# Strassen's algorithm for the memory side of the gate in a gated cross-attention kernel on one Trainium2 core

## The chip, the core and the metric

The kernel runs on one of the eight cores of one Trainium2 chip. A core has five engines that run beside each other and meet only through semaphores: TensorE (PE: matrix products and transposes into PSUM; its weight loads are shown as PEld), VectorE (DVE), ScalarE (ACT), GpSimd (POOL) and SyncE (SP, which here only issues DMAs). Each engine works through its own instructions in order, and so does the DMA queue of each. The metric is the device time of one execution in microseconds (us).

## The reference

```python
# x: (8, 1024, 1024)   memory (ctx_1024): (8, 64, 512)
memory_proj = einsum('bme,de->bmd', memory, W_mem)              # called mp below
scores = einsum('bnd,bmd->bnm', x, memory_proj) / sqrt(1024)
attn = softmax(scores, axis=-1)
memory_context = einsum('bnm,bmd->bnd', attn, memory_proj)
gate_input = concatenate([x, memory_context], axis=-1)
gate = sigmoid(einsum('bnf,df->bnd', gate_input, W_gate) + b_gate)
fused = x + gate * memory_context
out = fused * rsqrt(mean(fused**2, axis=-1) + 1e-6) * norm_w
```

All is float32. The kernel splits W_gate into W1 (the columns that meet x) and W2 (those that meet memory_context). As memory_context is attn times mp, its part of the gate is attn times (mp @ W2.T), so the kernel computes mp @ W2.T + b_gate once for all 8 x 64 = 512 memory rows, and calls it mg.

## The kernel before

**Setup** (lines 116 to 452), once. Five matmuls of zeros occupy TensorE until the first data is there. SP issues the loads in this order: mem in two tiles of 256 rows (`memq`), the rest of W_mem (`wm`; its first chunk is issued by ACT), the eight row chunks of W2 (`w2`), the bias, and W1 in two halves (`w1_0`, `w1_1`). TensorE transposes the first `memq` tile into PSUM (`transpose_mem`, line 182), DVE and ACT copy it to `memT`, and TensorE forms the first half-width products with W_mem for four of the eight output chunks (`mem_product` with 256 columns); then the same for the second tile, then the rest of W_mem's product at 512 columns. The eight results `pm` fill the eight PSUM banks. DVE copies each to `mpT` (line 237): mp transposed, features on partitions, 512 memory rows in the free dimension.

mp goes out to DRAM twice, to be loaded again per batch: as rows (`mgd[0]`, by DVE block transposes into `mpq` and 16 DMAs, lines 240 to 254) and transposed (`mpd`, lines 255 and 256). Then TensorE computes mp @ W2.T as 2 column halves x 4 row tiles, each a sum over 8 chunks (`pg`, lines 429 to 434). DVE adds the bias to each tile, and SP stores it to `mgd[1]`. Beside these eight tiles, DVE also forms the sums of W1's blocks (`w1_tasks`) and the first block of rows of x, transposed (`first`); POOL does only the `inner_s` sums of the first product.

**W1's sums.** x @ W1.T is done by Strassen's algorithm (Winograd's form) on two levels. The outer level has the products 1 to 7, in the order 1, 6, 7, 5, 4, 2, 3 (`ORDER`, line 465). Their right operands are blocks 1, 7, 2, 3 of W1 and three outer sums, blocks 5, 6, 4 (`outer_sum`, 128x2048 elements each). Inside each block there is a second level, which needs four sums of 128x512 (`inner_sums`). In the kernel before, those of blocks 1, 7, 5, 6, 4 are made in the setup, and those of blocks 2 and 3 in slots 2 to 13 of the loop (line 501).

**Loop** (lines 747 to 750): 16 blocks of 512 rows of x, each 49 slots, and seven outer products of seven inner products each. An inner product is a slot: two matmuls of 128x256. The order of everything else is written out by hand: `at(slot, ...)` puts work in front of a slot's matmuls, and `mid((q, o), ...)` puts it behind a product's fifth inner product. Each outer product uses five PSUM banks, A to E, and F takes B's. DVE empties B, C and D into `u`, and at the end adds the inner results into `gate` (`fin`); POOL does the additions that need no PSUM (`pre`) and the left operands' sums (`inner_s`). The banks rotate from product to product:

```python
banks = [banks[i] for i in (2, 3, 0, 4, 1)]
```

so the next product's A is the old C, its B the old D, and its C the old A. In products 5, 4, 2 and 3 the attention's part of the gate is added in the same banks.

All instructions of an engine stay in the order in which the program issues them (`keep_in_program_order`). Tiles with the same tag share a buffer: the next user waits until the last reader is done.

Of the kernel before, what the change touches and what calls it, by code (L numbers as in the profile page):

```python
# [8 lines left out]
F32 = mybir.dt.float32  # L9
AF = mybir.ActivationFunctionType  # L10
ALU = mybir.AluOpType
# [4 lines left out]
P = 128  # L16
# [4 lines left out]
def tile_gated_cross_attention_rmsnorm(  # L21
# [7 lines left out]
    norm_w: bass.AP,  # L29
    out: bass.AP,  # L30
):

# [28 lines left out]
    nc = tc.nc  # L63
# [8 lines left out]
    H = 512  # L72
# [17 lines left out]
    def mm(o, lhsT, rhs, start, stop):  # L90
        pin(nc.tensor.matmul(o, lhsT, rhs, start=start, stop=stop, skip_group_check=True))  # L91

    def tt(eng, o, a, b, op):
        pin(eng.tensor_tensor(o, a, b, op))  # L94

    def load(o, i):
        pin(nc.sync.dma_start(o, i))

    def t4k(pool, shape, tag, name):
        return pool.tile(shape, F32, tag=tag, name=name)  # L100

    def rows_by_chunk(w, n):

        return w.rearrange("(p j) f -> p j f", j=n)

    def chunks(t, n):

        return t.rearrange("p s e -> p (s e)").rearrange("p (m j) -> p j m", j=n)
# [3 lines left out]
    def bank(n, shape, name):  # L112
        return ps.tile(shape, F32, tag=banks[n % 5], name=name)
# [20 lines left out]
    for k in range(KD):  # L134
        t = t4k(*((gpool, [P, D], "gate") if k < 7 else (apool, [P, D], "s4")), f"w2_{k}")
        load(t, w2r[:, k, :])
        w2.append(t)
    bias_sb = t4k(small, [P, D], "junk", "bias_sb")
    load(bias_sb, b_gate.partition_broadcast(P))

    w1 = [const.tile([P, 4, D], F32, name=f"w1_{h}") for h in range(2)]
    for h in range(2):
        load(w1[h], rows_by_chunk(w_gate_t[:D, :], KD)[:, 4 * h : 4 * h + 4, :])
    xq = {}

    def load_xq(q):
        b, n0 = q // QPB, (q % QPB) * QT
        xq[q] = t4k(xqpool, [P, 16, Q4], "xq", f"xq{q}")  # L150
        src = x[b, n0 : n0 + QT, :].rearrange("(s c) (i e) -> i c s e", c=32, i=4)
        for i in range(4):
            load(xq[q][32 * i : 32 * (i + 1), :, :], src[i])
# [3 lines left out]
        o: w1[h][:, :, c * H : (c + 1) * H]  # L157
        for o, h, c in ((1, 0, 0), (7, 0, 1), (2, 1, 0), (3, 1, 1))
    }
    for o in (5, 6, 4):  # L160
        outer_b[o] = const.tile([P, 4, H], F32, name=f"t{o}")
    inner_t = {o: const.tile([P, 3, 2, C], F32, name=f"it{o}") for o in range(1, 8)}

    def w_op(o, s):
        if s >= T4:
            return inner_t[o][:, s - T4, :, :]
        k, n = {R11: (0, 0), R21: (1, 0), R12: (0, 1), R22: (1, 1)}[s]
        return outer_b[o][:, 2 * k : 2 * k + 2, n * C : (n + 1) * C]

    nw_sb = const.tile([P, D], F32, name="nw_sb")  # L170

    ident = const.tile([P, P], F32, name="ident")
    make_identity(nc, ident)
# [3 lines left out]

    mpd = dram.tile([P, KD, BM], F32, name="mpd")
    mgd = dram.tile([2, BM, D], F32, name="mgd")
    memT = [t4k(apool, [P, 2, BM], f"a1{i + 1}", f"memT{i}") for i in range(2)]  # L180

    def transpose_mem(g):

# [11 lines left out]
            o = memT[k // 2][:, k % 2, cols]  # L195
            pin((nc.scalar.copy if k % 2 else nc.vector.tensor_copy)(o, pt[k][:, cols]))

    mpT = [
        t4k(rot, [P, 2, BM], tag, f"mpT_{tag}_{i}")
        for tag in ("l2", "u")  # L200
        for i in range(2)
    ]

    def mp_rows(j, q):
        return mpT[j // 2][:, j % 2, q * P : (q + 1) * P]


    mpq = [t4k(apool, [P, 4, Q4], f"a{i}{j}", f"mpq{i}{j}") for i in (1, 2) for j in (1, 2)]
    pt = [bank(4, [P, BM], "pt0")]
    pt += [ps_ctx.tile([P, BM], F32, tag="ctx", name=f"pt{k}") for k in (1, 2)]  # L210
    pt += [ps.tile([P, BM], F32, tag="sc", name="pt3")]
    pm = [bank(j, [P, BM], f"pm{j}") for j in range(4)]

    def mem_product(j, k, cols=slice(0, BM)):
        mm(
            pm[j][:, cols],
            chunks(wm[:, k : k + 1, :], KD)[:, j],
            memT[k // 2][:, k % 2, cols],
            k == 0 and cols.start == 0,
            k == KE - 1,  # L220
        )


    for g in range(2):
        transpose_mem(g)
        for j in range(KD // 2):
            mem_product(j, 0, slice(g * (BM // 2), (g + 1) * (BM // 2)))
    pm.append(bank(4, [P, BM], "pm4"))
    pm += [ps_ctx.tile([P, BM], F32, tag="ctx", name=f"pm{j}") for j in (5, 6)]
    pm += [ps.tile([P, BM], F32, tag="sc", name="pm7")]  # L230
    for j in range(KD // 2, KD):
        mem_product(j, 0)
    for k in range(1, KE):
        for j in range(KD):
            mem_product(j, k)
    for j in range(KD):
        pin(nc.vector.tensor_copy(mpT[j // 2][:, j % 2, :], pm[j]))
    load_xq(0)
    load(nw_sb, norm_w.partition_broadcast(P))
    for g in range(4):  # L240
        for j in range(0, KD, 2):
            pin(
                nc.vector.transpose(
                    chunks(mpq[g], KD)[:, j : j + 2],
                    mpT[j // 2][:, :, g * P : (g + 1) * P],
                )
            )
        for i in range(4):
            load(
                mgd[0, g * P : (g + 1) * P, i * Q4 : (i + 1) * Q4].rearrange(  # L250
                    "(s c) e -> c s e", c=32
                ),
                mpq[g][32 * i : 32 * (i + 1), :, :],
            )
    for j in range(0, KD, 2):
        load(mpd[:, j : j + 2, :], mpT[j // 2])


    def outer_sum(o, a, b):
        tt(nc.vector, outer_b[o], outer_b[a], outer_b[b], ALU.subtract)  # L260

    def inner_sums(o):
        for s, a, b in ((T1, R12, R11), (T2, R22, T1), (R12, R22, R12), (T4, R21, T2)):
            yield lambda s=s, a=a, b=b: tt(
                nc.vector, w_op(o, s), w_op(o, a), w_op(o, b), ALU.subtract
            )


    w1_tasks = [
        lambda: outer_sum(5, 7, 1),  # L270
        *inner_sums(1),
        lambda: outer_sum(6, 3, 5),
        lambda: outer_sum(7, 3, 7),
        *(f for o in (7, 5) for f in inner_sums(o)),
        lambda: outer_sum(4, 2, 6),
        *(f for o in (6, 4) for f in inner_sums(o)),
    ]
    w1_last = [f for o in (2, 3) for f in inner_sums(o)]


    A, S, L2, O = {}, {}, {}, {}
    sTs, attns, attnTs, scs, mps, mgs = {}, {}, {}, {}, {}, {}
    KH = KD // 2

    def where(q, t=0):
        return q // QPB, (q % QPB) * QT + t * P

    def transpose_x(q, t, half):

        key = q, t // 2, half  # L290
        if key not in A:
            A[key] = t4k(
                apool, [P, KH, 2 * P], f"a{t // 2 + 1}{half + 1}", f"a{t // 2 + 1}{half + 1}_{q}"
            )
        r = t % 2
        pin(
            nc.vector.transpose(  # L297
                A[key][:, :, r * P : (r + 1) * P],
                chunks(xq[q][:, 4 * t : 4 * t + 4, :], KD)[:, half * KH : (half + 1) * KH],
            )  # L300
        )

    def outer_s(q, n):
        a11, a12, a21, a22 = (A.get((q, r, h)) for r in range(2) for h in range(2))
        if n == 3:
            S[q, 3] = a21
            tt(nc.vector, a21, a11, a21, ALU.subtract)
            return
        s = S[q, n] = t4k(apool, [P, KH, 2 * P], f"s{n}", f"s{n}_{q}")
        if n == 1:  # L310
            tt(nc.vector, s, a21, a22, ALU.add)
        elif n == 2:
            tt(nc.vector, s, S[q, 1], a11, ALU.subtract)
        else:
            tt(nc.vector, s, a12, S[q, 2], ALU.subtract)
# [95 lines left out]
    def load_mp(b):  # L411
        mps[b] = t4k(small, [P, KD, M], "mpb", f"mpb{b}")
        load(mps[b], mpd[:, :, b * M : (b + 1) * M])

    def load_mg(b):
# [2 lines left out]
            load(mgs[b][g * M : (g + 1) * M, :], mgd[g, b * M : (b + 1) * M, :])  # L418


    first = [
        *(lambda t=t: transpose_x(0, t, 0) for t in (0, 1)),
        *(lambda t=t, h=h: transpose_x(0, t, h) for h in range(2) for t in (2, 3)),
        lambda: outer_s(0, 1),
        lambda: outer_s(0, 2),
        *(lambda t=t: transpose_x(0, t, 1) for t in (0, 1)),
    ]
    done, n = 0, 0
    for h in range(2):
        cols = slice(h * H, (h + 1) * H)  # L430
        for q in range(NPAIR):
            pg = bank(n, [P, H], f"pg2_{h}_{q}")
            for k in range(KD):
                mm(pg, mp_rows(k, q), w2[k][:, cols], k == 0, k == KD - 1)
            stage = t4k(small, [P, H], ("mg", "attnT", "mpb")[n % 3], f"g2_{h}_{q}")
            tt(nc.vector, stage, pg, bias_sb[:, cols], ALU.add)
            load(mgd[1, q * P : (q + 1) * P, cols], stage)
            if n < 5:
                while done < len(w1_tasks) * (n + 1) // 5:
                    w1_tasks[done]()  # L440
                    done += 1
            if n == 4:
                for f in first[:2]:
                    f()
                for part in range(2):
                    inner_s(0, 1, part)
            elif n == 5:
                for f in first[2:]:
                    f()
            n += 1  # L450
    load_mp(0)
    load_mg(0)


# [43 lines left out]
            at(t0 + 10, load_mp, (q + 1) // QPB)  # L498
            at(t0 + 49, load_mg, (q + 1) // QPB)

    for i, fn in enumerate(w1_last):
        at((2, 3, 4, 5, 10, 11, 12, 13)[i], fn)
    slot = 0

    def step():
# [274 lines left out]
```

## Time and profile before

Three runs: 989.25, 989.34 and 990.49 us, median 989.34. The profiled execution took 990.88 us; its span, from the first instruction to the last, is 989.1 us, and the granted TensorE clock 0.995 of full.

| stretch of the span, us | what TensorE does | DVE busy | POOL busy |
|---|---|---|---|
| 0 to 6.67 | zeros, and waits for mem | little | little |
| 6.67 to 12.3 | mem's transposes, first half-width products | 1.7 us | none |
| 12.3 to 38.4 | W_mem's product | idle 19.9 us before the first copy | none |
| 38.4 to 93.4 | mp @ W2.T | 4 to 5 of each 5 us from 35 to 65, then 3.2 to 5 up to 90 | from 88.5 only |
| 93.4 to the end | the loop, 16 x 56 us | 2.4 to 5 of each 5 us | 2.1 to 5 of each 5 us from 100 on |

The page gives the busy time of each engine and the chain of work that ended last: from the last instruction back to whatever released it. A line such as `38.58 54.93 PE pg L91 x128` reads: from 38.58 us on, for 54.93 us, 128 records of TensorE writing tile `pg`, recorded at line 91 (all matmuls go through one helper). A matmul on FP32 operands shows as two records. `[0.84 <-DMA memq<-in_mem]` at a line's end means that the engine had been idle for 0.84 us, and that this load ended the wait.

### The profile page before, as it was taken

To read this page: it belongs to the slowest core of one execution; us is meant where nothing else is said; L and a number is where in the kernel's file an instruction comes from. 1 tells how busy PE (TensorE), PEld (TensorE's weight loads), DVE (VectorE), ACT (ScalarE), POOL (GpSimd) and SP (SyncE) were. 2 spreads that over 40 slices of the span, in tenths; PEclk is the share of its full clock that TensorE was granted. 3 is DMA by queue.
4 is the path that set the end of the run, shared out by engine and by line. 5 is a ranking of instruction groups with operands and counts; after the bars stand their busy time and mean duration, and the time that the engine had idled before them with its cause. 6 is when DMAs were issued, how large, how long until landed. Compare 5 with 4: busy or idle time off the path is not lost.

```text
span 989.1 us, 14267 instructions
## 1 busy us (share of the span) xinstructions
PE 974.1 (98%) x4962; PEld 775.8 (78%) x4962; DVE 810.3 (82%) x1491; ACT 321.7 (33%) x592; POOL 688.1 (70%) x851
## 2 busy tenths in 40 slices
PE   9999999999999999999999999999999999999994
PEld 7545788888888888888887888888887888888873
DVE  0677787979798897979798897979797988979787
ACT  1000115233333415142342424152333334151434
POOL 0002777878787787878787887878787887868772
PEclk9999999999999999999999999999999999999998
DMA  9772537191926556281927465381918364472612
GB/s 367 200 239 71 90 58 167 54 202 64 168 80 130 125 119 148 71 188 61 182 85 130 115 127 131 85 192 48 197 65 154 103 137 109 102 176 66 169 65 85
DMA packets 69160, 126.76 MB, mean 128 GB/s; under 512 B 12384, under 2 KB 47200, under 8 KB 68704
## 3 DMA queue, kind: packets, MB, share of 16 engines
q1 hardware_dynamic: 60304, 93.86, 35.0%
q0 software_dynamic: 8640, 31.46, 17.3%
q8 instruction: 39, 0.64, 0.3%
q10 hardware_dynamic: 144, 0.52, 0.2%
q14 instruction: 33, 0.27, 0.1%
HBM read 85.98 MB, written 39.85 MB: 127 GB/s over the span
## 4 chain that ended last, share of the span: by engine, by line
PE 96%; DVE 2%; DMA 1%; issue 0%; ACT 0%; POOL 0%; DVEq 0%; ACTq 0%
PE kA L91 19%; PE pc L91 12%; PE kE L91 11%; PE kF L91 10%; PE kD L91 10%; PE kC L91 10%; PE kB L91 10%; PE psT L91 6%; PE pg L91 6%; PE pm L91 3%; DVE gate L94 1%; DMA memq<-in_mem 1%; DVE gate L594 0%; PE pa L391 0%; PE sc L365 0%
## 5 line engine op out<-in xcount | busy, mean ns | idle before, releaser
L94 POOL TENSOR_TENSOR gate<-gate,u 128x256 f32<-128x256 f32 x336 | 270.5, 835 | 123.3 <-DVE u L94 123.3
L94 POOL TENSOR_TENSOR l<-a 128x256 f32<-128x256 f32 x128 | 128.5, 1004 | 151.5 <-PE pg L91 87.1
L516 ACT ACTIVATE gate<-gate 128x512 f32<-128x512 f32 x128 | 79.2, 631 | 399.8 <-DVE gate L94 399.8
L297 DVE STREAM_TRANSPOSE a<-xq 128x512 f32<-128x512 f32 x128 | 138.0, 1100 | 0.0
L91 PE MATMUL pc<-mg,attnT 64*128 64x256 f32 x512 | 127.4, 389 | 0.0
L545 DVE SCALAR_TENSOR_TENSOR gate<-gate,ss,nw_sb 128x512 f32<-128x512 f32 x120 | 126.1, 1061 | 1.1
L91 PE MATMUL kB<-it,l 128*128 128x256 f32 x448 | 115.0, 379 | 0.0
L91 PE MATMUL kD<-it,l 128*128 128x256 f32 x448 | 115.0, 379 | 0.0
L91 PEld LDWEIGHTS pc<-mg,attnT 64*128 64x128 f32 x512 | 90.6, 186 | 29.7 <-issue 21.2
L91 PE MATMUL kA<-w,a 128*128 128x256 f32 x384 | 98.7, 379 | 0.4 <-ACT u L660 0.4
L91 PEld LDWEIGHTS kB<-it,l 128*128 128x128 f32 x448 | 85.1, 190 | 11.6
L91 PEld LDWEIGHTS kD<-it,l 128*128 128x128 f32 x448 | 85.1, 190 | 11.6
L94 DVE TENSOR_TENSOR gate<-gate,pc 128x512 f32<-128x512 f32 x128 | 87.3, 682 | 5.9 <-ACT gate L516 5.9
L660 ACT COPY u<-kA 128x256 f32<-128x256 f32 x112 | 40.6, 363 | 142.2 <-PE kA L91 140.0
L91 PEld LDWEIGHTS kA<-w,a 128*128 128x128 f32 x384 | 71.6, 190 | 10.2 <-ACT u L660 0.8
L94 POOL TENSOR_TENSOR l<-s 128x256 f32<-128x256 f32 x96 | 75.5, 786 | 1.6 <-PE kF L91 1.5
L94 DVE TENSOR_TENSOR u<-u,kB 128x256 f32<-128x256 f32 x112 | 45.6, 408 | 30.1 <-PE kB L91 26.0
L91 PE MATMUL kE<-it,a 128*128 128x256 f32 x256 | 69.0, 392 | 0.0
L91 PE MATMUL kA<-t,s 128*128 128x256 f32 x256 | 67.4, 386 | 0.0
L91 PE MATMUL kC<-w,l 128*128 128x256 f32 x256 | 65.7, 379 | 0.0
L91 PE MATMUL kF<-w,l 128*128 128x256 f32 x256 | 65.7, 379 | 0.0
L530 ACT ACTIVATE junk<-gate 128x1024 f32<-128x1024 f32 x60 | 63.6, 1060 | 1.6 <-DMA gate<-in_x 0.6
(107 smaller groups left out, 1959.5 us busy)
## 6 DMA issues: line engine op xcount, KB each, us to landing
xq<-in_x SPq DMA_DIRECT2D x64, 512.0 KB, 9.7
gate<-in_x POOLq DMA_DIRECT2D x60, 512.0 KB, 8.9
out<-gate SPq DMA_DIRECT2D x60, 512.0 KB, 2.6
w<-in_w_gate_t SPq DMA_DIRECT2D x8, 512.0 KB, 11.3
w<-in_w_gate_t SPq DMA_DIRECT2D x2, 2048.0 KB, 16.2
mg<-mgd SPq DMA_DIRECT2D x16, 256.0 KB, 4.1
mgd<-mpq SPq DMA_DIRECT2D x16, 128.0 KB, 2.7
mgd<-g SPq DMA_DIRECT2D x8, 256.0 KB, 2.2
```

What stands on the lines that cost most here:

```text
L91: pin(nc.tensor.matmul(o, lhsT, rhs, start=start, stop=stop, skip_group_check=True))
L94: pin(eng.tensor_tensor(o, a, b, op))
L297: nc.vector.transpose(A[key][:, :, r * P : (r + 1) * P], chunks(xq[q][:, 4 * t : 4 * t + 4, :], KD)[:, half * KH : (half + 1) * KH],)
L516: pin(nc.scalar.activation(g, g, AF.Sigmoid))
L530: nc.scalar.activation(junk, O[q, t], AF.Square, accum_out=ss[:, t % 2 : t % 2 + 1])
L545: nc.vector.scalar_tensor_tensor(g[:, cols], g[:, cols], rstd[:, t % 2 : t % 2 + 1], nw_sb[:, cols], ALU.mult, ALU.mult,)
L660: pin(nc.scalar.copy(p1, kb["A"]))
```

## The change

It does five things.

1. `mem` is wholly transposed before W_mem's product starts; that product then runs at 512 columns throughout. `memT` moves to other buffers.
2. `pm` is copied in two halves of 256 rows, one by DVE, one by ACT, into four tiles `mpT[r][h]` (row half r, feature half h: m11, m12, m21, m22).
3. mp @ W2.T is done by one step of Strassen's algorithm: seven products of 256x512 by 512x512, in the order 1, 6, 5, 2, 7, 4, 3. Each has two row tiles of four matmuls. W2's sums are t1, t2, then b12 and b21 in place; mp's are s1, s2, s3, and s2 once more. The results are combined in c11, c12, c21 and c22 on DVE. The bias is added once to c11, c12 and c21 (c22 takes it from c12) by POOL.
4. POOL also takes b12's sums, s3, the second s2, and the inner sums of W1's blocks 7 and 6. Those of blocks 5 and 4 move into the loop with those of 2 and 3: 16 sums in slots 3 to 23.
5. The loads of the bias and of norm_w are issued behind W1. The rows of mp are stored (`store_mp`) between the products, and `load_mp(0)` in their middle.

```diff
-    for g in range(2):
-        transpose_mem(g)
-        for j in range(KD // 2):
-            mem_product(j, 0, slice(g * (BM // 2), (g + 1) * (BM // 2)))
...
+    for g in range(2):
+        transpose_mem(g)
+    pm = [bank(j, [P, BM], f"pm{j}") for j in range(5)]
...
+    for k in range(KE):
+        for j in range(KD):
+            mm(
+                pm[j],
+                chunks(wm[:, k : k + 1, :], KD)[:, j],
+                memT[k // 2][:, k % 2, :],
...
-    for j in range(KD):
-        pin(nc.vector.tensor_copy(mpT[j // 2][:, j % 2, :], pm[j]))
...
-    for h in range(2):
-        cols = slice(h * H, (h + 1) * H)
-        for q in range(NPAIR):
-            pg = bank(n, [P, H], f"pg2_{h}_{q}")
-            for k in range(KD):
-                mm(pg, mp_rows(k, q), w2[k][:, cols], k == 0, k == KD - 1)
-            stage = t4k(small, [P, H], ("mg", "attnT", "mpb")[n % 3], f"g2_{h}_{q}")
-            tt(nc.vector, stage, pg, bias_sb[:, cols], ALU.add)
-            load(mgd[1, q * P : (q + 1) * P, cols], stage)
...
+    w2_sum(nc.vector, t1, b12, b11)
+    w2_sum(nc.vector, t2, b22, t1)
+    w2_sum(nc.gpsimd, b12, b22, b12)
+    w1_place(5)
+    outer_sum(5, 7, 1)
+    inner_sums(nc.vector, 1)
...
+    mpT = [[t4k(apool, [P, KH, HM], f"a{r + 1}{h + 1}", f"mpT{r}{h}") for h in range(2)] for r in range(2)]
+    for j in range(KD):
+        for r, copy in ((0, nc.vector.tensor_copy), (1, nc.scalar.copy)):
+            pin(copy(mpT[r][j // KH][:, j % KH, :], pm[j][:, r * HM : (r + 1) * HM]))
+    (m11, m12), (m21, m22) = mpT
...
+    def mg_product(n, l, r):
+        nonlocal mg_next
+        pgs = []
+        for t in range(2):
+            tag = mg_banks[mg_next % 8]
+            mg_next += 1
+            pg = (ps_ctx if tag == "ctx" else ps).tile([P, H], F32, tag=tag, name=f"pg{n}_{t}")
+            for k in range(KH):
+                mm(pg, l[:, k, t * P : (t + 1) * P], r[k], k == 0, k == KH - 1)
+            pgs.append(pg)
+        return pgs
...
+    def mg_sum(o, a, pgs):
+        for t in range(2):
+            tt(nc.vector, o[:, t, :], a[:, t, :], pgs[t], ALU.add)
...
+    s1 = mp_step(nc.vector, "s1", apool, m21, m22, ALU.add)
+    s2 = mp_step(nc.vector, "s2", apool, s1, m11, ALU.subtract)
+    outer_sum(7, 3, 7)
+    w1_place(7)
+    s3 = mp_step(nc.gpsimd, "l2", rot, m11, m21, ALU.subtract)
+    for n in range(4):
+        inner_sum(nc.gpsimd, 7, n)
...
+    pgs = mg_product(1, m11, b11)
+    for t in range(2):
+        pin(nc.scalar.copy(c11[:, t, :], pgs[t]))
+    store_mp(2)
+    store_mp(3)
+    pgs = mg_product(6, s2, t2)
+    mg_sum(c21, c11, pgs)
+    store_mp(0)
+    tt(nc.gpsimd, s2, m12, s2, ALU.subtract)
+    pgs = mg_product(5, s1, t1)
+    mg_sum(c12, c21, pgs)
+    mg_bias(nc.gpsimd, c12, 1)
+    store_mp(1)
+    w1_place(6)
+    outer_sum(6, 3, 5)
     load_mp(0)
+    pgs = mg_product(2, m12, b21)
+    mg_sum(c11, c11, pgs)
+    mg_bias(nc.gpsimd, c11, 0)
+    store_mg(c11, 0, 0)
+    w2_sum(nc.vector, b21, b21, t2)
+    w1_place(4)
+    outer_sum(4, 2, 6)
+    for n in range(4):
+        inner_sum(nc.gpsimd, 6, n)
+    pgs = mg_product(7, s3, b12)
+    mg_sum(c22, c12, pgs)
+    mg_sum(c21, c21, pgs)
+    store_mg(c22, 1, 1)
+    for t in range(2):
+        transpose_x(0, t, 0)
+    for part in range(2):
+        inner_s(0, 1, part)
+    for t in (2, 3):
+        transpose_x(0, t, 0)
+    pgs = mg_product(4, m22, b21)
+    mg_sum(c21, c21, pgs)
+    mg_bias(nc.gpsimd, c21, 0)
+    store_mg(c21, 1, 0)
+    for t in (2, 3):
+        transpose_x(0, t, 1)
+    outer_s(0, 1)
+    for t in range(2):
+        transpose_x(0, t, 1)
+    pgs = mg_product(3, s2, b22)
+    mg_sum(c12, c12, pgs)
+    store_mg(c12, 0, 1)
+    outer_s(0, 2)
     load_mg(0)
...
-    for i, fn in enumerate(w1_last):
-        at((2, 3, 4, 5, 10, 11, 12, 13)[i], fn)
+    for o in (2, 3):
+        w1_place(o)
+    for i, (o, n) in enumerate((o, n) for o in (5, 4, 2, 3) for n in range(4)):
+        at(
+            (3, 4, 5, 6, 10, 11, 12, 13, 14, 15, 17, 18, 19, 20, 22, 23)[i],
+            inner_sum,
+            nc.vector,
+            o,
+            n,
+        )
```

`w2_sum` is four subtractions of 128x512, one for each chunk; `mp_step` is one of 128x1024; `mg_bias` is two additions of 128x512; `store_mp(g)` is two DVE block transposes of 128x512 and four DMAs; `store_mg` is one DMA of 512 KB.

## The prediction

> **What bounds the kernel now.** I read the busy times first, then the chain that ended last, then that chain in order of time.
>
> ```profile
> span 989.1 us, 14267 instructions
> PE 974.1 (98%) x4962; PEld 775.8 (78%) x4962; DVE 810.3 (82%) x1491; ACT 321.7 (33%) x592; POOL 688.1 (70%) x851
> PE 96%; DVE 2%; DMA 1%; issue 0%; ACT 0%; POOL 0%; DVEq 0%; ACTq 0%
> ...
> 8.62 2.88 PE pm L91 x8
> 11.50 0.96 PE pt L189 x8
> 12.46 26.11 PE pm L91 x64
> 38.58 54.93 PE pg L91 x128
> 93.51 0.86 PE kA L91 x4
> ```
>
> The chain is TensorE for 96%; its own waits add up to 3.6 us in the whole run. So time goes only if TensorE loses work, and comes only if TensorE is made to wait. The change rewrites the stretch from 8.6 to 93.4 us. In it `pg` is a block without a gap: 54.93/128 = 0.429 us for each pass of 512 columns. An FP32 matmul is two records here, so one matmul costs 0.858 us.
>
> **Part 1: seven products for eight.** Before: 8 tiles x 8 matmuls = 64. After: 7 products x 2 row tiles x 4 = 56 of the same shape (128x128 against 512). 8 x 0.858 = **6.87 us** go, if the products follow each other. With T for the end of `pm`, product n starts at T + 6.87(n-1), and the loop at T + 48.1. Their inputs, laid out on DVE and POOL by rows of the trace (DVE sums 0.61 us apart for 128x512, about 1.15 for 1024 and 2.2 for 2048; stream transposes 1.02; sums with a PSUM input 0.61 to 0.68):
>
> - The W2 loads are ahead of W1 and bias in the queue and land by about 22 us (the last is issued near 11.7 and takes 10.2), so `t1` and `t2` (8 x 0.61) end near 23. `w1_0` is issued 1.2 us earlier (the bias load was in front) and lands near 26.8, not 28; then `outer_sum(5)` and the four sums of block 1 take 2.2 + 2.4, to 31.5. The first `pm` is ready to copy near 32, and DVE idled until 32.6 before: free. At 3 us later the `m11` copies would still be in time.
> - The eight copies (DVE 0.42, ACT 0.37, beside each other) keep up with one `pm` per 0.86 us. s1 and s2 are ready at T + 3; product 6 needs them at T + 6.9.
> - POOL has no 128x512 row; two 128x256 passes at their 0.69 spacing give 1.38, 1024 elements 2.76. s3 ends near T + 0.5 (needed T + 27.5), b12 before 30 us, the second s2 near T + 16.5 (needed T + 41.2).
> - The b21 sums on DVE start when product 2 ends (T + 27.5) and its sums are done, about T + 28.2, and end at T + 31 to 33; product 4 needs them at T + 34.4. This is the tightest on DVE.
> - Handover: `outer_sum(4)` ends near T + 33.5 to 35.5; POOL then has the four sums of block 6 (5.5), four sums of `inner_s(0,1)` (2.8), needed near T + 49, and done at T + 44. Queued behind them are c21's bias (2.8), its store (2.2 to landing for a smaller one; I take 2.5), and the `inner_s(0,6)` sums, which reuse c21's buffer: T + 50.4, needed T + 58.6.
> - DVE's `mg_sum(c12)`, `outer_s(0,2)` end near T + 51; the first DVE add of the loop could start at T + 49.8. The four slots until product F reads that bank again cover the 1.3 us, and DVE idled 1.47 us at the score product.
>
> DMA: SP waits in order for c11's bias, c22, c21, c12 and c12's landing before `load_mg(0)`, so the load of the next x goes out some 6 us into the loop, not 3.3. It takes about 10 us, and is used 26 us in. `load_mp` is past by T + 25. Nothing waits.
>
> **Part 2: mem transposed first.** Here the order of records matters.
>
> ```profile
> 6.67 1.95 PE L189 MATMUL pt<-ident,memq 128*128 128x128 f32 x8 [0.84 <-DMA memq<-in_mem]
> 8.42 3.08 PE L91 MATMUL pm<-memT,wm 128*128 128x256 f32 x8
> 11.34 1.13 PE L189 MATMUL pt<-ident,memq 128*128 128x128 f32 x8
> 12.30 26.28 PE L91 MATMUL pm<-memT,wm 128*128 128x256 f32 x64
> ```
>
> In windows of a tenth of a microsecond, transposes start 0.214 us apart up to 8.2, the half-width passes 0.43 apart up to 10.55 and 0.24 or less after that; the second transposes are 0.12 apart. The array runs at half pace until about 10.6, although the granted-clock row reads 1.0. After: the second memory tile landed at 1.2 + 6.6 = 7.8, so its eight transposes run from 8.4 at 0.214, to 10.1. Then 64 full passes, 64 x 0.429 = 27.5; half a microsecond at half pace costs 0.25. T = 10.1 + 27.5 + 0.25 = 37.8, against 38.42: **0.6 us** gained. The Trainium skill, "TensorE: Matmul & The Clock Gate", Part 1, says that the full clock comes after a busy window of 3.4 us that runs free of the kernel. By that, 10.6 can move by a window from run to run; by the row it stays. I keep the row, and 0 to 1.0 as ends.
>
> **Part 3: eight sums moved into the loop.** Blocks 5 and 4, eight sums of 128x512, leave the setup's DVE work; with blocks 2 and 3 there are 16 in slots 3 to 23, where 8 were in slots 2 to 13. The eight new ones are in slots 14 to 23, on a full DVE:
>
> ```profile
> 109.64 1.23 DVE L94 TENSOR_TENSOR w<-w 128x512 f32<-128x512 f32 x1
> 110.80 0.41 DVE L94 TENSOR_TENSOR gate<-gate,kE 128x256 f32<-128x256 f32 x1
> 111.13 0.88 DVE L94 TENSOR_TENSOR it<-w,it 128x512 f32<-128x512 f32 x1
> ...
> 112.93 0.41 DVE L94 TENSOR_TENSOR gate<-gate,kF 128x256 f32<-128x256 f32 x1
> 113.26 0.41 DVE L94 TENSOR_TENSOR u<-u,kB 128x256 f32<-128x256 f32 x1
> ```
>
> kF of product 6 ended about 109.5 and is evacuated at 112.93: DVE is some 3 us behind before anything is added. The four sums of slots 10 to 13 took 0.68, 0.79, 1.23 and 0.88, against 0.69 alone: mean 0.90, about 0.81 apart. Bank D of one outer product becomes bank B of the next. From 113.26 there are five adds at 0.34 to D's last, so 114.96, plus four new sums ahead of it. At 0.81 that is 118.2, and kB of product 5 wants the bank at 116.86: **1.3 us** of stall. From there to the same point of product 5 there are four more sums (3.2), five adds (1.7), the attention difference (0.4), two transposes (2.04) and four adds (1.3): 126.9. kB of product 4 wants it at 125.03 + 1.3 = 126.3: **0.6** more. After that DVE idles about 3 us between 128 and 133 and catches up. Together 1.9.
>
> A rule speaks against this part and against POOL's new share. "SBUF — State Buffer", Who interferes with whom: a DVE instruction with two SBUF inputs contends with a GpSimd one that reads SBUF, and whichever issues second is fully blocked. POOL is busy 4.24 and 4.92 us of 5 in 110:115 and 115:120. By the rule each new sum waits for half a POOL sum, 0.61 + 0.37 = 0.98, and the same count gives 2.0 + 1.3 = 3.3. At the uncontended 0.61 it gives 0.5. Part of the blocking is in this row, which comes from this very loop, so I take the row's 1.9 and keep 0 to 3.3. In the setup the rule bites little: `mg_sum` has a PSUM input and transposes have one input, so only c12's and c11's biases and c21's meet DVE sums, some 2 us later in all, inside the slacks above.
>
> **The sum.** 6.87 + 0.6 - 1.9 = 5.6 us less. The profiled execution took 990.88, span 989.1 and 1.8 around it: a span near 983.5. On the median of the runs, 989.34 - 5.6 = **983.7 us**.
>
> **Rivals.**
>
> A, likeliest, 0.60: as summed, 982.3 to 985.3.
>
> B, 0.17: the loop's added sums are hidden, because POOL and DVE interleave better than in slots 10 to 13; 989.34 - 7.5 = 981.9. For it: later blocks of rows run with extra norm instructions on DVE and TensorE hardly waits. Against: only about three of those fall in slots 0 to 24, and eight are added here.
>
> C, 0.13: the handover costs 2 us too, for instance b21 or c21's bias late, beside the dear end of Part 3: 989.34 - 7.5 + 5.3 = 987.1, spread from 985.3 to 989. For it: the tight b21 slack. Against: 4 to 8 us of slack elsewhere.
>
> D, 0.08, slower: POOL's chain at the handover. From T + 35.5 it does 12.4 us of sums at a stretch factor f and a store of 2.5 until `inner_s(0,6)`, so TensorE waits 12.4f - 20.6. This begins at f = 1.66; 7.5 us are eaten, the loop's loss aside, at f = 2.27, a 128x512 POOL sum of 3.1 us. At f = 2.5 it waits 10.4: 989.34 - 7.5 + 10.4 + 1.9 = 994.1. For it: single POOL sums of 1.64 beside a DVE sum, 2.4 times 0.69. Against: the worst group of POOL sums has a mean of 1004 ns, f = 1.45, and most DVE work at that place is transposes.
>
> E, 0.02: the products go no faster, because the passes lengthen with the new operands: 989. Against: the same shapes, and a weight load (0.19 us) under the 0.43 of a pass.
>
> **Numbers.** What a measurement here can tell from no change is about 0.2%, 2.0 us: under 987.4 is faster, over 991.3 slower. Faster: A, B and 0.09 of C = 0.86. Same: 0.04 of C and E = 0.06. Slower: D, 0.08. The range joins the ends, best start with nothing lost in the loop, 989.34 - 6.87 - 1.0 = 981.5, to C's middle, 987.1; a little wider, 981.2 to 987.3.
>
> **What would show it.** `pg` with 112 records at 0.429, without a gap; the loop's first kA near 85.9, not 93.35. `pm` starting near 10.1 as one run of 64 passes. TensorE waits of 0.5 to 3.3 us in outer products 5 and 4 of the first block of rows, with DVE adds as releasers, and none later. I am wrong if a product waits for POOL or for b21, if the first kB waits for `inner_s`, or if kB of product 5 finds its bank free.

## The result, and the profile after

The changed kernel takes **985.07 us** (median of 6 runs, 984.92 to 986.23) against 989.32 (6 runs beside it, 989.25 to 990.80): 4.25 us less, a ratio of 0.9956 with a 95% interval of 0.9943 to 0.9969. The profiled execution took 986.23 us, its span is 984.4, 4.7 less than before.

The page's first lines and its chain by engine, after:

```profile
span 984.4 us, 14254 instructions
PE 968.4 (98%) x4938; PEld 771.3 (78%) x4938; DVE 823.4 (84%) x1495; ACT 324.9 (33%) x602; POOL 722.2 (73%) x871
PE 95%; DVE 2%; POOL 1%; DMA 1%; issue 0%; ACT 0%; DVEq 0%; ACTq 0%
```

TensorE has 24 records less: 16 for the eight matmuls that went, 8 because mem's half-width products are whole. POOL is in the chain now with 1%, where it was at 0%. The chain in order of time shows where (start, length, what):

```profile
6.66 3.66 PE pt L196 x16
10.32 27.76 PE pm L92 x64
38.08 48.07 PE pg L92 x112
86.15 0.86 PE kA L92 x4
...
107.95 0.43 DVE u L95
108.37 0.07 issue
108.44 2.93 POOL gate L95 x3
111.37 1.14 POOL l L95
112.51 0.04 issue
112.55 1.13 PE kC L92 x4
...
116.60 4.17 POOL gate L95 x6
120.77 0.70 POOL l L95
121.51 1.13 PE kC L92 x4
```

`pg` is 48.07 us without a gap, where it was 54.93. At 86 us the changed kernel is 7.4 us ahead. Then the chain leaves TensorE twice in the first block of rows, for DVE and POOL, in products 7 to 4 of the loop. What TensorE itself waited for, in the whole run (total, times, longest):

```profile
PE kA L92 <- ACT u L740: 1.7, 3, 1.1
PE pz L92 <- DVE zeros L118: 1.2, 1, 1.2
PE kB L92 <- DVE gate L95: 0.9, 1, 0.9
PE pt L196 <- DMA memq<-in_mem: 0.8, 1, 0.8
PE kC L92 <- POOL l L95: 0.8, 2, 0.6
```

The third and fifth line are new. The table sets the same records of both profiles side by side (starts, us; the lead is the difference).

| record | before | after | lead |
|---|---|---|---|
| first `pg` | 38.42 | 37.92 | 0.50 |
| loop's first kA | 93.35 | 85.99 | 7.36 |
| product 7, kF | 115.14 | 107.98 | 7.16 |
| product 5, kB | 116.86 | 110.82 | 6.04 |
| product 5, kC | 117.72 | 112.55 | 5.17 |
| product 4, kB | 125.03 | 120.23 | 4.80 |
| product 4, kC | 125.89 | 121.51 | 4.38 |
| product 2, first kA | 132.34 | 128.06 | 4.28 |
| next block's scores | 154.81 | 150.53 | 4.28 |
| last block's scores | 925.46 | 921.18 | 4.28 |

So the setup gained 7.36 us, and 3.08 of them were lost again within 42 us of the loop, nothing after that until the last block. In that block 0.33 more went, and the time from the last DVE instruction's end to the end of the span is 0.7 shorter.

### The profile page after: what moved, and what is told of

Its sections match the earlier page's. It is cut to its first block, busy times and chain, and to the rows that moved or that the text cites. A ratio compares the mean times of both kernels' runs of the same rounds, so it can differ in the third digit from the quotient of the medians.

```text
span 984.4 us, 14254 instructions
## 1 busy us (share of the span) xinstructions
PE 968.4 (98%) x4938; PEld 771.3 (78%) x4938; DVE 823.4 (84%) x1495; ACT 324.9 (33%) x602; POOL 722.2 (73%) x871
## 4 chain that ended last, share of the span: by engine, by line
PE 95%; DVE 2%; POOL 1%; DMA 1%; issue 0%; ACT 0%; DVEq 0%; ACTq 0%
PE kA L92 19%; PE pc L92 11%; PE kE L92 11%; PE kD L92 10%; PE kC L92 10%; PE kF L92 10%; PE kB L92 9%; PE psT L92 6%; PE pg L92 5%; PE pm L92 3%; DVE gate L95 1%; POOL gate L95 1%; DMA memq<-in_mem 1%; DVE gate L674 0%; DVE u L95 0%
## 5 line engine op out<-in xcount | busy, mean ns | idle before, releaser
L92 PEld LDWEIGHTS kA<-w,a 128*128 128x128 f32 x384 | 71.6, 190 | 10.2 <-ACT u L740 0.8
## 6 DMA issues: line engine op xcount, KB each, us to landing
mpd<-mpT SPq DMA_DIRECT2D x4, 512.0 KB, 11.7
```

## The experiments

Each was run beside the kernel before, on one of two chips; that took 989.31 us in the median on the first and 989.20 on the second. The changed kernel was not run again there, so the differences from its 985.07 us are across chips. They are between medians unless a profile is named. The experiments ask three things: whether the added sums alone cost the 3 us, which of them and through which engine, and what the other parts were worth.

**The sums alone, in the kernel before.** The inner sums of blocks 5 and 4 leave the setup for the loop; nothing else is changed.

```diff
-        *(f for o in (7, 5) for f in inner_sums(o)),
+        *inner_sums(7),
         lambda: outer_sum(4, 2, 6),
-        *(f for o in (6, 4) for f in inner_sums(o)),
+        *inner_sums(6),
-    w1_last = [f for o in (2, 3) for f in inner_sums(o)]
+    w1_last = [f for o in (5, 4, 2, 3) for f in inner_sums(o)]
-        at((2, 3, 4, 5, 10, 11, 12, 13)[i], fn)
+        at((3, 4, 5, 6, 10, 11, 12, 13, 14, 15, 17, 18, 19, 20, 22, 23)[i], fn)
```

> The kernel before, with Part 3 alone: the inner sums of W1's blocks 5 and 4 leave the setup and go into slots 3 to 23 of the loop, as in the changed kernel. Theory (the eight added DVE sums alone cause the loop's loss): 989.3 + 3.1 = 992.4 us, with waits of TensorE at kB and kC of product 5 and at kC of product 4 in the first block of rows. Rival (the loss comes from how the new setup hands over to the loop: DVE late, POOL late, loads late): 989.3, no waits there.

Measured: 994.12 us median, 992.46 to 994.29; 1.0038 (1.0026 to 1.0051). Its runs fall in two groups, 992.5 to 992.7 and 994.1 to 994.3, and so do those of the kernel before, 989.2 to 989.3 and 990.5 to 990.8 (of which more below). Group against group the sums cost 3.3 to 3.5. The lower group lies where the theory put the time (992.4); the median is in the upper one because three of the five runs are. Its profile has the same waits as the changed kernel's:

```profile
PE kB L91 <- DVE gate L94: 0.9, 1, 0.9
PE pt L189 <- DMA memq<-in_mem: 0.8, 1, 0.8
PE kC L91 <- POOL l L94: 0.8, 2, 0.6
```

No part of the new setup is there, and the loss is. The handover is out as its cause.

**The sums of blocks 2 and 3 later**, in the changed kernel:

```diff
-            (3, 4, 5, 6, 10, 11, 12, 13, 14, 15, 17, 18, 19, 20, 22, 23)[i],
+            (3, 4, 5, 6, 10, 11, 12, 13, 22, 23, 29, 30, 31, 32, 33, 34)[i],
```

> The changed kernel, with the sums of blocks 2 and 3 in slots 22, 23 and 29 to 34, where DVE idled about 3 us before, and not in 14 to 23. Theory (the crowding in slots 14 to 23): the 3.1 us of waits in products 7, 5 and 4 go, 985.1 - 2.5 to 3.1 = 982.0 to 982.6; a new lag in product 2 could give a part back. Rival (handover): 985.1.

Measured: 982.34 us (982.11 to 982.50); 0.9925 (0.9912 to 0.9937). That is 2.7 us below the changed kernel: the same sums, placed where DVE had idle time, are all but free. From the loop's first kA to the first kA of product 2 its profile takes 39.11 us; the kernel before takes 38.99 there and the changed kernel 42.07. TensorE's waits on DVE and POOL in the loop are gone from its profile. It beats both kernels.

**POOL's order.** In the first block of rows, the second half of `inner_s` for products 5 and 4 is put ahead of the additions that wait for DVE:

```diff
-            for part, t in ((0, 1), (1, 5)):
+            for part, t in ((0, 1), (1, 2 if q == 0 and i in (2, 3) else 5)):
```

> The changed kernel, with one edit in POOL's queue: in the first block of rows, the second half of inner_s for products 5 and 4 stands ahead of the pre additions (slots 16 and 23, not 19 and 26). Theory (part of the loss is POOL's order: those sums stand behind additions that wait for a late DVE): the waits of kC in products 5 and 4, 0.6 + 0.2 us in the records and about 1.3 to 1.7 in lost time, go, and the wait of kB (0.9) stays: about 983.6. Rival (only DVE's lag counts, POOL's order just shows it): 985.1, the time lost at kC comes back at another bank.

Measured: 984.89 us (984.83 to 985.00); 0.9951 (0.9937 to 0.9965): against 985.07, no change that can be told. TensorE's waits in it:

```profile
PE kB L92 <- DVE gate L95: 0.9, 1, 0.9
PE kF L92 <- DVE u L95: 0.5, 1, 0.5
PE kD L92 <- DVE u L95: 0.3, 1, 0.3
```

The wait for POOL is gone, and two waits for DVE stand in its place. From the loop's first kA to the first kA of product 2 it takes 126.70 - 84.63 = 42.07 us, and the changed kernel 128.06 - 85.99 = 42.07 as well. So the rival has the time right: the loss comes back at other banks. But the edit did not leave DVE alone. The second of the added sums took 1.10 us here, beside POOL's moved ones, and 0.69 in the changed kernel, and bank D of product 7 was empty 25.2 us into the loop, not 24.8. What POOL's order would be worth with DVE undisturbed is therefore open.

**Which four sums.** Two complements: block 2's sums late and block 3's left in place, and the other way round.

```diff
-            (3, 4, 5, 6, 10, 11, 12, 13, 14, 15, 17, 18, 19, 20, 22, 23)[i],
+            (3, 4, 5, 6, 10, 11, 12, 13, 29, 30, 31, 32, 19, 20, 22, 23)[i],
```

> The changed kernel, with block 2's four sums alone moved from slots 14, 15, 17, 18 to 29 to 32; block 3's stay in 19, 20, 22, 23. By the prediction's count (the four sums ahead of bank D's last add in product 7 are the costly ones): bank D is free at 114.96 on the old scale, before kB of product 5 asks for it at 116.86, D of product 5 at 123.7, before 125.03: no wait of TensorE in products 5 and 4, 982.3 us. Rival (any eight sums before slot 24 cost the same): half of the 2.7 us that late sums gave back, 983.7.

Measured: 982.22 us (982.11 to 983.15); 0.9930 (0.9917 to 0.9942). Banks D are free in time, as expected, but "no wait" is not quite so: kC of product 5 starts 1.16 us behind kB in its profile, and not 0.86, as its left operand comes late from POOL. The other:

```diff
-            (3, 4, 5, 6, 10, 11, 12, 13, 14, 15, 17, 18, 19, 20, 22, 23)[i],
+            (3, 4, 5, 6, 10, 11, 12, 13, 14, 15, 17, 18, 29, 30, 31, 32)[i],
```

> The complement: block 3's four sums moved from slots 19, 20, 22, 23 to 29 to 32; block 2's stay in 14 to 18. By the count: kB of product 5 still waits (1.3 us), kC of product 5 with it (about 0.9 more), product 4 no longer: 982.3 + 1.3 to 2.2 = 983.6 to 984.5. Rival (any eight sums cost the same): 983.7, as in the other one; then the two do not differ.

Measured: 983.76 us (983.71 to 984.73); 0.9946 (0.9934 to 0.9958). Its waits on the loop's banks:

```profile
PE kB L92 <- DVE gate L95: 0.9, 1, 0.9
PE kC L92 <- POOL l L95: 0.2, 1, 0.2
```

This time is that of the theory and of the rival alike; only the pair tells them apart. The two differ by 1.5 us, so the number of sums before slot 24 is not what counts. With four sums in slots 19 to 23 alone, the stretch from the loop's first kA to product 2 takes 39.38 us, 0.4 more than in the kernel before, and the time is that of the run with all eight late. Four in slots 14 to 18 cost 1.5 more, and those in 19 to 23 another 1.3 (985.07 - 983.76) once the first four have made DVE late.

**mem's transposes.** The old order is put back in the changed kernel:

```diff
     for g in range(2):
         transpose_mem(g)
+        for j in range(KD // 2):
+            mem_product(j, 0, slice(g * (BM // 2), (g + 1) * (BM // 2)))
...
+    for j in range(KD // 2, KD):
+        mem_product(j, 0)
+    for k in range(1, KE):
+        for j in range(KD):
+            mem_product(j, k)
```

> The changed kernel, with Part 2 undone: mem is transposed in two parts with half-width products of W_mem between them. Theory: pm ends at 38.4, not 37.9, and the time is 0.5 us longer, 985.6. Rival (the start's half-pace phase hides it): 985.1, no change.

Measured: 985.19 us (985.07 to 986.47); 0.9956 (0.9943 to 0.9968). Against 985.07 that is 0.1 us, within what the runs scatter. Neither expectation is excluded by its interval alone. The next part tells why the profile promised more.

**Full pace from the start.** The profiles taken in this case show two kinds of start. The chain's start in the changed kernel, and in the one with all eight sums late (start, length):

```profile
2.63 3.19 PE L92 MATMUL pz<-zeros 128*128 128x256 f32 x7
6.66 3.66 PE L196 MATMUL pt<-ident,memq 128*128 128x128 f32 x16 [0.83 <-DMA memq<-in_mem]
10.11 2.22 PE L92 MATMUL pm<-memT,wm 128*128 128x512 f32 x4
```

```profile
2.64 2.44 PE L92 MATMUL pz<-zeros 128*128 128x256 f32 x7
6.76 2.53 PE L196 MATMUL pt<-ident,memq 128*128 128x128 f32 x16 [1.69 <-DMA memq<-in_mem]
9.13 3.35 PE L92 MATMUL pm<-memT,wm 128*128 128x512 f32 x7
```

The code up to there is the same in both. In the second the array has come to full pace among the zeros, the 16 transposes take 2.53 us and not 3.66, and the loop starts at 84.84, not 85.99. Of the profiled executions of this case five start late (both kernels, the one with the sums alone, the one with mem's old order, the one with the stores behind), and their times are of the upper group of their kernel's runs; five start early, and theirs are not. To test this, the kernel before got seven matmuls of zeros for five, which closes most of the gap before mem arrives (0.18 us of 0.84 is left in its profile):

```diff
-    for _ in range(5):
+    for _ in range(7):
         mm(pz, zeros[:, :P], zeros, True, True)
```

> The kernel before, with seven matmuls of zeros at the start, not five. Its runs fall in two groups, 989.2 to 989.3 and 990.5 to 990.9; the profiled one was of the second, with half pace until 10.6 us. Theory (the array comes to full pace after a busy stretch of its own free-running windows; the 0.84 us gap between zeros and mem spoils one): with the gap closed, full pace comes early in every run, all runs lie within 989.0 to 989.6. Rival (the two groups come from something else): the groups stay, about two runs in five at 990.5 to 991, and each run is up to 0.9 us longer for the two matmuls more if they push mem's transposes back.

Measured: 989.40 us over 11 runs, 989.08 to 989.71; 0.9999 (0.9990 to 1.0008). None of the 11 is in the upper group, where 3 of the 15 runs beside it were. With those odds 11 runs miss the group by chance about once in twelve ((12/15)^11 = 0.09); and as 3 of 15 is a small sample itself, chance is nearer one in six (3 upper runs dealt at random among the 26 all fall among the 15 in 455 of 2600 ways). So this supports the theory and does not prove it. Two runs (989.70 and 989.71) lie above the forecast 989.6. The median isn't better: what the upper group loses is avoided, and the lower group, 989.2 in the median, loses 0.2.

This profile starts early with mem in the old order, so the two starts can be set beside the two orders. From mem's first transpose to the first `pg` it takes 30.20 us, and the four early profiles with the new order 30.01 to 30.14. Of the late ones, the three with the old order take 31.68 to 31.75, and the two with the new one 30.97 and 31.26. So transposing mem first is worth 0.4 to 0.8 us after a late start, and 0.1 to 0.2 after an early one.

**The stores in front.** In the changed kernel the four stores of mp transposed stand in SP's queue ahead of those of mp's rows. They are moved behind:

```diff
-    for r in range(2):
-        for h in range(2):
-            load(mpd[:, h * KH : (h + 1) * KH, r * HM : (r + 1) * HM], mpT[r][h])
...
     outer_sum(6, 3, 5)
+    for r in range(2):
+        for h in range(2):
+            load(mpd[:, h * KH : (h + 1) * KH, r * HM : (r + 1) * HM], mpT[r][h])
     load_mp(0)
```

> The changed kernel, with the four stores of mp transposed (11.7 us to landing in the trace) issued behind the stores of mp's rows, not ahead of them. In the changed kernel DVE idles 4.9 us for those row stores and the b21 sums end at 72.3, the moment product 4 starts. Theory: DVE's idle goes, b21 ends some 4 us earlier, and the time stays 985.1, because nothing waited for it. Rival (the setup's late DVE is carried into the loop and is part of the loss there): 984 or less.

Measured: 984.90 us (984.83 to 985.95); 0.9957 (0.9944 to 0.9971). DVE's idle is gone, and the time is the same. The same four stores now land in 4.9 us, not 11.7. But half of the theory fell: the b21 sums end at 71.6, hardly earlier than 72.3. In the changed kernel, then in this one (DVE):

```profile
57.49 2.04 DVE L419 STREAM_TRANSPOSE mpq<-mpT 128x512 f32<-128x512 f32 x2 [4.87 <-DMA mgd<-mpq]
...
66.19 6.11 DVE L95 TENSOR_TENSOR w<-w,t_w 128x512 f32<-128x512 f32 x4
```

```profile
52.22 2.05 DVE L416 STREAM_TRANSPOSE mpq<-mpT 128x512 f32<-128x512 f32 x2
...
65.88 5.71 DVE L95 TENSOR_TENSOR w<-w,t_w 128x512 f32<-128x512 f32 x4
```

These sums start when product 2 has ended, and are slow in themselves: 1.4 to 1.5 us each, where 0.69 is their length alone.

## Why the prediction came out as it did

It said 983.7 us, 5.6 less; measured were 985.07 and 4.25 less. The direction, the place of the loss and its first cause were right. Two terms were mis-sized, both too favourably: Part 2 by 0.5 us, and Part 3, in its second half, by 0.8 in the medians (1.2 in the profile). The measured time lies at the dear end of the likeliest case, A.

**Part 1** held: 6.87 us predicted, 54.93 - 48.07 = 6.86 in the profiles. No product waited. The work of DVE and POOL beside the products fitted as laid out, with two exceptions that cost nothing. "Nothing waits" on DMA was wrong: DVE waited 4.87 us for the row stores, behind the transposed stores, which took 11.7 us to land (3.8 to 5.0 before). With these moved behind, the wait and the 11.7 are gone, and the time stays: it was spare time. And "in the setup the rule bites little" was wrong for b21: its four sums met POOL's bias and block 6's sums, both with two SBUF inputs as its own, and took 6.11 us, not 2.4. They ended at 72.30, and product 4 was due at 37.92 + 5 x 6.87 = 72.27. The forecast of T + 31 to 33 became T + 34.4. Here the Trainium skill's rule ("SBUF — State Buffer", Who interferes with whom) was the better guide: a DVE sum of 0.69 that waits out most of a POOL sum of 1.28 us comes to the 1.75 that three of the four took (the first took 1.09). Still nothing waited. Product 4's first matmul started at 72.25, ahead of the last sum's end: each of its four matmuls for a row tile reads one chunk of b21, so the last chunk was needed some 2.6 us (3 x 0.858) after the first. That slack of about 2.5 us, which the prediction did not count, took up the delay.

**Part 2**: 0.6 predicted, 0.50 in the two profiles, 0.1 in the medians. The step that failed is "I keep the row". The two profiles compared are both of the upper group of runs, with half pace until about 10 us or later, and there the working was right (0.4 to 0.8 above). Most runs are of the lower group, where the array is at full pace before mem arrives, and there the new order gains only 0.1 to 0.2. The skill's rule that I had beside it ("TensorE: Matmul & The Clock Gate", Part 1: the window runs free of the kernel, so the moment moves from run to run) agrees with the two starts shown above, and should have set the value for a median, since one profile shows one such moment only.

**Part 3**: 1.9 predicted; 3.08 in the profile, 2.7 to 2.9 given back by the two kernels with the sums placed later, 3.3 to 3.5 in the kernel before with the sums alone. By its steps:

- The first stall, bank D of product 7 asked for by kB of product 5, was put at 1.3 us. The lead falls by 1.32 there, from 7.36 to 6.04 (0.20 of it already at kF of product 7). Bank D was due to be empty 24.85 us into the loop, 118.2 on the old scale, and was at 24.78: the first line below is DVE's last add to it, and kB starts as it ends. The two complements confirm the choice of the four sums ahead of that bank as the costly ones.
- The second stall was put at 0.6, at kB of product 4. From product 5's kB to product 2's first kA, 6.04 - 4.28 = 1.76 us were lost, in two parts. Up to product 4's kB it is 1.24, 0.6 more than predicted, and DVE's lag alone would account for that: D of product 5 was due to be empty 33.6 us into the loop, and was at 34.2 (the second line). The eight sums took 0.89, 0.69, 0.68, 0.89, 1.23, 0.88, 1.12 and 0.88 us. Start to start the first four came 0.74 apart on average, and the last four 0.95, where the prediction has 0.81 for all. The dearer count that it worked out and set aside has 0.98 per sum and 3.3 in all (its terms add up to 3.2); with 3.08 in the profile, that was the nearer.

```profile
110.36 0.41 DVE L95 TENSOR_TENSOR gate<-gate,kD 128x256 f32<-128x256 f32 x1
...
119.43 0.74 DVE L95 TENSOR_TENSOR gate<-gate,kD 128x256 f32<-128x256 f32 x2
```

  The other 0.5 came behind product 4's kB, most of it (4.80 - 4.38) at kC. It shows what the prediction left out altogether, POOL. These are the same waits at product 5 (TensorE's view, then POOL's):

```profile
110.82 1.13 PE L92 MATMUL kB<-it,l 128*128 128x256 f32 x4 [0.87 <-DVE gate L95]
112.55 1.13 PE L92 MATMUL kC<-t,l 128*128 128x256 f32 x4 [0.61 <-POOL l L95]
```

```profile
108.44 2.93 POOL L95 TENSOR_TENSOR gate<-gate,u 128x256 f32<-128x256 f32 x3 [2.21 <-DVE u L95]
111.33 1.17 POOL L95 TENSOR_TENSOR l<-s 128x256 f32<-128x256 f32 x1
```

  POOL sat idle for 2.21 us until DVE gave it the `u` of kC; its three additions came next, and behind them, in order, the sum that is the left operand of product 5's kC. TensorE waited for that. The same again at product 4 (six additions, 4.17 us, then `l`). Of the 1.7 us of new waits in the records POOL released 0.8, where the prediction named DVE adds alone. It moved DVE's lag from bank to bank, and never asked who else waits for the late `u`. POOL was late because DVE was, so this queue is first of all a place where the lag comes out: with its order changed, the loss came out at kF and kD instead. Whether the order adds something of its own, that run does not show.

**The rivals.** B, that the sums are hidden, fell; it becomes true at 982.2 to 982.3 when the sums are moved. C's late handover and D's chain on POOL did not occur: POOL's 128x512 sums took 1.28 alone and at most 1.79 beside DVE, 1.30 times the 1.38 that f = 1 stood for, and `inner_s` for the first product was done at 82.1, 4 us before the loop. The dear end of Part 3, which C had beside its handover (3.3), came close. E fell with Part 1.

The balance in medians: 6.87 for the products, 0.1 for mem, less 2.7 for the sums: 4.3, measured 4.25. In the profiles: 7.36 less 3.08, less 0.33 in the last block, plus 0.7 in the last stores: 4.7, as the spans show. Where the 0.33 and the 0.7 come from was not tried.

## What to carry to other kernels

Work that is taken off a busy stretch and put "beside" the bound engine is only free where the helper engine is on time: count its lag at the place, not its mean share (DVE was at 82%, and 3 us behind just there), and move the work to a stretch with idle time; here that was worth 2.7 us of the 7 that the change could give. When one engine is late, list everything that its late results release, on every other in-order queue, before pricing the lag. And a term that hangs on the start's clock needs more than one profile: one trace shows one start.

## What the runs showed of the hardware that was not expected

- TensorE comes to full pace at different moments in different runs of one program: among the zeros, before 6.7 us, or near 10.6. In ten profiles this goes with two groups of times some 0.8 to 1.6 us apart (989.2 to 989.3 and 990.5 to 990.8 before; 984.9 to 985.1 and 985.9 to 986.2 after). The granted-clock row reads 1.0 in both.
- Four DVE sums of 128x512 beside POOL sums took 6.11 us, 1.53 each against 0.69 alone, more than anything the loop showed (1.23 at most before).
- POOL sums of 128x512 take 1.28 us and of 128x1024 2.35, which is 1.75 and 3.2 times the 0.73 of 128x256.
- The time of a store to landing depended on when it was issued. The four stores of mp transposed (512 KB each, rows of 1 KB) took 11.7 us when they were issued right behind the load of x, at 40 to 46 us, and 4.9 when issued at 63 to 65 us. In the kernel before, the same data in rows of 2 KB took 3.8 to 5.0 at 57 to 59 us, and stores of 128 KB, issued behind the load of x at 41 to 45 us, took some 11. So the 11.7 is not due to the shorter rows.
